# Four layers on one core: Newton's steps in PSUM, the sums' reciprocals as a tenth tap, and a ring of four pools

## The chip, the cores and the metric

The kernel runs on one core of a Trainium2 chip. The metric is the device time of that core in microseconds, as the median of several runs. One execution more was taken with the hardware profiler; all lines of a profile come from it. The engines are TensorE (PE; its weight loads are listed as PEld), VectorE (DVE), ScalarE (ACT), GpSimd (POOL) and SyncE (SP), whose queue issues the DMAs here.

## The reference

Two images of 512 channels and 64 x 64 points pass through four layers; each layer normalises its input by groups, computes, and adds the result to what came in. The change touches the first and the third.

```
x = x + L0(gn(x));  x = x + L1(gn(x));  x = x + L2(gn(x));  x = x + L3(gn(x))

def L0(x):                                # 8 heads of 64, window 3 x 3
    q = x @ W_q + b_q;  k_l, v_l = split(x @ W_kv + b_kv)
    q_norm = q / max(|q|, 1e-12);  k_l = k_l / max(|k_l|, 1e-12)     # per head
    q_scaled = (q_norm + query_embedding) * softplus(temperature)
    attn_local = q_scaled . (k_l at the 9 taps around the point)
    attn_pool  = q_scaled . normalised keys of 256 pooled tokens
    a_local, a_pool = softmax([attn_local, attn_pool])               # one sum for both
    lt = q_norm . learnable_tokens + learnable_bias + a_local
    xo = sum over 9 taps(lt * v_l at the tap) + a_pool . v_pool
    return xo @ W_proj + b_proj

def L2(x):
    gap = mean of x over the points
    s = relu(relu(gap @ w1 + b1) @ w2 + b2)          # one number per channel
    pools = [max over k x k windows of x for k in (1, 3, 5, 7, 9, 11, 13)]
    return the two pools next to s, mixed linearly, + x
```

## The kernel before

Both images run the same program one after the other: 128 channels or tokens lie on the partitions, and the four channel chunks of an image are tiles of 128 x 4096. All matmuls are in float32. Instructions of one engine run in the order in which the program was written down; a tile framework adds the semaphores between engines.

**First layer, class Local.** The work is cut into 16 units, a chunk of 128 channels (two heads) by 1024 points each. A loop over units puts the stages of neighbouring units side by side: `projections` (keys four units ahead, queries three, values one), `norms` for what was projected in the round before, `tap_products` and `tap_sums` for the next unit, `attend` for the present one, `weigh` for the one before. Each stage is a generator; `in_turn` calls them in turn, one step up to the next `yield` from each, and this fixes the order on every engine by hand. The tile pool "mm" has five PSUM banks, which `bank()` hands out to all stages.

In `norms`, four matmuls sum squares by head (L2003), ScalarE copies the rows (L2006), TensorE transposes them (L2010), and VectorE computes the inverse square root of 128 x 32 numbers: a bound below (L2013), a first guess by integer shift and multiply (L2017, L2018), a factor (L2019), and three Newton steps of three instructions (L2021, L2022, L2024); the last writes into the tile `wide`. TensorE transposes `wide` back (L2029). `normed` spreads the result over channels (L2043) and multiplies keys and queries (L2051).

In `attend`, exponentials of the scores against the pooled tokens go to `values` (L2146; GpSimd adds pairs of them, L2151) and to `sums` (L2158, L2162), whose reciprocals VectorE writes into `recip` (L2183). `el` holds the exponentials of the nine tap scores in rows of 32 per head and tap; it is multiplied by the reciprocals and the learned part is added (L2186, L2187). It then goes to DRAM, and every tap's row is fetched back, repeated over the 64 channels of its head (`fetch_tap`, L2200), because a row must meet channels that lie on the partitions.

In `weigh`, the attention over the pooled tokens, `out`, is first multiplied by the reciprocals, spread by two matmuls (L2213, L2216). Then for each of nine taps ScalarE copies the fetched rows into two PSUM banks (L2223), VectorE multiplies the shifted values by them and writes into the tap's buffer (L2226), and GpSimd adds the buffer to `out` (L2230). Three tap buffers go round: tap k + 3 is fetched when tap k is added. At the end `out` is stored to DRAM (`yd`, L2236).

**Third layer.** `pool_weights` takes group means and variances of the four chunks (L87 to L99, with GpSimd's power for the inverse root), the gap, two small matmuls (L647, L653) and almost 40 small VectorE instructions for the mixture of each channel (L656 to L680). `pool_chunk` builds the six pools of a chunk, each from the one before: a 3 x 3 maximum is a horizontal one into `h` and a vertical one into `p` (`spread_max`, L692, with an edge copy by ScalarE, L693; the first pool needs two more, L1161 and L1163). Two `h` and two `p` go round. TensorE adds each pool to eight PSUM banks by a matmul with a diagonal matrix (`add`, L1151 and L1153), which needs the mixture.

Of the kernel before, what the change touches and what calls it, by code (L numbers as in the profile page):

```python
# [15 lines left out]
P = 128  # L16
C = 512
KC = C // P
W = 64
# [38 lines left out]
class General:  # L58
# [578 lines left out]
    def pool_weights(self, X, w1, w2, sp, pp, mv=None):  # L637
# [6 lines left out]
        nc.vector.tensor_tensor(gap, gap, rstd, ALU.mult)  # L644
        ps = pp.tile([P, TB], F32, name="mm")
# [34 lines left out]
        nc.vector.tensor_scalar(c0, c0, 1.0, None, ALU.add)  # L680
# [247 lines left out]
class Net(General):  # L928
# [208 lines left out]
    def pool_weights(self, X, w1, w2, sp, pp):  # L1137
        return super().pool_weights(X, w1, w2, sp, pp, self.mv)

    def pool_chunk(self, X, Y, cc, c0, d0, wts, sp, ppa):  # L1140
# [5 lines left out]
        tmp = [Y[:, i, :].rearrange("p (y x) -> p y x", x=W) for i in range(KC)]  # L1146
# [10 lines left out]
        for j in range(1, 7):  # L1157
            h, p = tmp[j % 2], tmp[2 + j % 2]
            if j == 1:
                self.spread_max(h, img, 2)  # L1160
                nc.vector.tensor_tensor(h, h, img, ALU.max)  # L1161
                self.spread_max(p, h, 1)
                nc.vector.tensor_tensor(p, p, h, ALU.max)  # L1163
            else:

                self.spread_max(h, tmp[2 + (j - 1) % 2], 2)
                self.spread_max(p, h, 1)
            add(wts[:, j, cc:cc + 1], Y[:, 2 + j % 2, :], j)
# [491 lines left out]
class Local:  # L1660
# [332 lines left out]
    def norms(self, streams, ended):  # L1993
# [15 lines left out]
        for t in range(NT):  # L2009
            nc.tensor.transpose(ps[:, t * P:(t + 1) * P], rows[:, t * P:(t + 1) * P],  # L2010
                                self.net.ident)
        n, y, a = (wp.tile([P, NT, 4, 2], F32, name=f"norms{i}") for i in range(3))
        nc.vector.tensor_scalar(n, ps.rearrange("p (t s r) -> p t s r", t=NT, s=4)[:, :, :, :2],  # L2013
                                1e-24, None, ALU.max)
        yield

        nc.vector.tensor_scalar(y.bitcast(I32), n.bitcast(I32), 1, None, ALU.logical_shift_right)  # L2017
        nc.vector.tensor_scalar(y.bitcast(I32), y.bitcast(I32), -1, 0x5f3759df, ALU.mult, ALU.add)  # L2018
        nc.vector.tensor_scalar(n, n, -0.5, None, ALU.mult)  # L2019
        for i in range(3):  # L2020
            nc.vector.tensor_tensor(a, y, y, ALU.mult)  # L2021
            nc.vector.tensor_tensor(a, a, n, ALU.mult)  # L2022
            dst = self.wide.rearrange("p t (s r) -> p t s r", s=4)[:, :, :, :2] if i == 2 else y
            nc.vector.scalar_tensor_tensor(dst, a, 1.5, y, ALU.add, ALU.mult)  # L2024
        yield
# [97 lines left out]
    def attend(self, u):  # L2123
# [67 lines left out]
        self.fetch_tap(0)  # L2191
        yield
        self.fetch_tap(1)
        yield

    def fetch_tap(self, k):

        at = 32 * (k % 2) + 2 * k
        for h in range(2):
            self.nc.sync.dma_start(self.taps[k % 3][h * HD:(h + 1) * HD, :],  # L2200
                                   bcast(self.spread[at + h], 0, HD))

    def weigh(self, u):
# [3 lines left out]
        out, R = self.out.pop(u), self.recip  # L2207
        self.fetch_tap(2)
        yield
        banks = [self.bank() for _ in range(2)]  # L2210
        for j, ps in enumerate(banks):
            q = slice(64 * j, 64 * j + 2)
            nc.tensor.matmul(ps, self.cst[q, C_ROW:C_ROW + P], R[q, :], start=True, stop=True)  # L2213
        for j, ps in enumerate(banks):
            o = out[:, j * TB:(j + 1) * TB]
            nc.vector.tensor_tensor(o, o, ps, ALU.mult)  # L2216
        for k in range(9):
            dy, dx = divmod(k, 3)
            parts = [self.taps[k % 3][:, j * TB:(j + 1) * TB] for j in range(2)]

            banks = [self.bank() for _ in range(2)]
            for ps, part in zip(banks, parts):
                nc.scalar.copy(ps, part)  # L2223
            for j, (ps, part) in enumerate(zip(banks, parts)):
                y = y0 + dy + j * self.UY // 2
# [4 lines left out]
            nc.gpsimd.tensor_tensor(out, out, self.taps[k % 3], ALU.add)  # L2230
            if k + 3 < 9:
                self.fetch_tap(k + 3)
            if k < 8:
# [165 lines left out]
```

## Time and profile before

| | us |
|---|---|
| median of 10 runs | 5610.08 (5604.83 to 5619.77) |
| the profiled execution | 5608.33 |
| its span, first to last instruction | 5606.5 |
| first layer, image 1 and image 2 | 0 to 1148, 2800 to 3929 |
| third layer, image 1 and image 2 | 1625 to 1907, 4408 to 4690 |
| TensorE's granted clock, mean | 0.961 of full speed |

All times inside the profile are counted from the start of the span, so the span is compared with positions, and the profiled execution's own time with the runs. In a line of the timeline stand the start, the duration, the engine, the line of the kernel, the operation, the tiles written and read, and in brackets how long the engine had been idle and who released it. A row can take several instructions together ("x4").

### The profile page before, as it was taken

The numbers are of one execution on the slowest core, as the hardware profiler recorded it, in microseconds if no ns is written. First come the engines' busy times: TensorE is split into PE (matmuls) and PEld (weight loads), VectorE is DVE, ScalarE is ACT, GpSimd is POOL, SyncE is SP. The second block draws the span as 40 slices with busy tenths as digits, with TensorE's granted clock in tenths as the row PEclk, the third lists the DMA queues.
The fourth block names the chain that finished last, engine by engine and source line by source line (L and its number), as shares of the span: only waits on it lengthen the run. The fifth ranks groups of instructions, "written<-read, shape, count | busy, mean of one in ns | idle before, by whom it ended". The sixth has DMA issues, their size and how long they took to land.

```text
span 5606.5 us, 51804 instructions
## 1 busy us (share of the span) xinstructions
PE 5240.1 (93%) x19291; PEld 2263.0 (40%) x19291; DVE 3176.3 (57%) x3816; ACT 1790.4 (32%) x3413; POOL 1812.2 (32%) x1196
## 2 busy tenths in 40 slices
PE   7899999999978899999998999989999789999999
PEld 4333332554323444544343332325543334445443
DVE  3257777745669633544432677777456695334444
ACT  1245555333212233212212455542332122332221
POOL 0025555501310045444400455554013101453443
PEclk9899999999989999999998999999999899999999
DMA  3024444500000000200010344454000000000000
GB/s 137 0 64 118 123 114 136 167 21 24 1 1 0 1 1 1 76 19 34 31 51 2 87 114 116 115 148 143 17 24 1 1 0 1 1 8 14 18 15 24
DMA packets 103354, 276.37 MB, mean 49 GB/s; under 512 B 15091, under 2 KB 28147, under 8 KB 101045
## 3 DMA queue, kind: packets, MB, share of 16 engines
q1 hardware_dynamic: 103092, 272.97, 16.6%
q8 instruction: 154, 2.52, 0.2%
q14 instruction: 108, 0.88, 0.1%
HBM read 224.68 MB, written 48.23 MB: 49 GB/s over the span
## 4 chain that ended last, share of the span: by engine, by line
PE 72%; DVE 15%; issue 5%; DMA 3%; POOL 2%; ACT 2%; SPq 0%; DVEq 0%; POOLq 0%; ACTq 0%
PE mm L133 25%; DVE big L692 6%; PE mm L1330 4%; PE mm L1615 4%; PE mm L1370 4%; PE mm L547 4%; PE mm L1226 2%; PE mm L1410 2%; PE psO L1242 2%; PE psO L1602 2%; PE mm L1933 2%; PE mm L1631 2%; PE tap L2104 2%; DVE big L2226 2%; POOL late L2230 1%
## 5 line engine op out<-in xcount | busy, mean ns | idle before, releaser
L133 PE MATMUL mm<-big,w 128*128 128x512 f32 x2560 | 1200.2, 613 | 6.6 <-DVE late L2183 5.1
L133 PEld LDWEIGHTS mm<-big,w 128*128 128x128 f32 x2560 | 470.1, 193 | 708.6 <-issue 602.2
L2230 POOL TENSOR_TENSOR late<-late,big 128x1024 f32<-128x1024 f32 x192 | 454.4, 2367 | 335.7 <-DVE big L2226 332.2
L1153 PE MATMUL acc<-big,dg 128*128 128x512 f32 x896 | 408.7, 615 | 79.2 <-DVE big L692 51.2
L692 DVE TENSOR_TENSOR big<-big 128x3968 f32<-128x3968 f32 x96 | 410.8, 4289 | 39.0 <-ACT big L693 17.2
L1232 POOL TENSOR_TENSOR total<-prob 128x512 f32<-128x512 f32 x128 | 159.7, 1269 | 759.5 <-ACT prob L1229 759.5
L1584 POOL TENSOR_SCALAR qf_sum<-qf,ksum_ratio 128x512 f32<-128x512 f32 x128 | 199.1, 1564 | 552.0 <-ACT qf L1634 351.5
L1405 POOL TENSOR_TENSOR big<-big 128x512 f32<-128x512 f32 x224 | 277.5, 1271 | 235.4 <-ACT big L1396 235.4
L2151 POOL TENSOR_TENSOR late<-late 128x512 f32<-128x512 f32 x128 | 160.7, 1277 | 503.1 <-ACT late L2140 477.8
L1609 DVE RECIPROCAL k<-psD 128x512 f32<-128x512 f32 x64 | 214.9, 3357 | 184.8 <-PE psD L1606 184.8
L1153 PEld LDWEIGHTS acc<-big,dg 128*128 128x128 f32 x896 | 174.0, 197 | 312.4 <-issue 283.4
L2223 ACT COPY mm<-big 128x512 f32<-128x512 f32 x384 | 221.7, 594 | 198.8 <-DMA big<-rows 105.9
L1396 ACT ACTIVATE big<-mm,ed 128x256 f32<-128x256 f32 x512 | 194.2, 490 | 276.5 <-DVE top L1392 248.7
L2226 DVE TENSOR_TENSOR big<-big,mm 128x512 f32<-128x512 f32 x384 | 252.4, 680 | 30.4 <-ACT mm L2223 26.9
L2230 POOL TENSOR_TENSOR late<-late,tap 128x1024 f32<-128x1024 f32 x96 | 228.1, 2376 | 123.1 <-DVE norms L2024 72.3
L1330 PE MATMUL mm<-proj,k 64*128 64x256 f32 x2048 | 265.1, 391 | 0.9 <-ACT k L1297 0.9
L1249 DVE RECIPROCAL recip<-psD 128x512 f32<-128x512 f32 x64 | 214.9, 3358 | 87.1 <-PE psD L1246 87.1
L2091 DVE TENSOR_TENSOR prod<-qs,big 128x1024 f32<-128x1024 f32 x192 | 230.9, 1218 | 42.9 <-PE tap L2104 42.6
L1551 DVE TENSOR_REDUCE tops<-mm 128x2 f32<-128x512 f32 x256 | 159.4, 681 | 163.4 <-PE mm L1330 163.3
L1229 ACT ACTIVATE prob<-mm 128x512 f32<-128x512 f32 x256 | 132.0, 604 | 364.4 <-PE mm L1226 359.2
L1330 PEld LDWEIGHTS mm<-proj,k 64*128 64x128 f32 x2048 | 207.6, 188 | 95.0 <-issue 78.7
L1615 PE MATMUL mm<-k,w 128*128 128x512 f32 x512 | 235.6, 602 | 0.0
(352 smaller groups left out, 8388.8 us busy)
## 6 DMA issues: line engine op xcount, KB each, us to landing
big<-rows SPq DMA_DIRECT2D x384, 256.0 KB, 4.0
tap<-rows SPq DMA_DIRECT2D x192, 256.0 KB, 4.0
yd<-late SPq DMA_DIRECT2D x32, 512.0 KB, 4.1
out<-big SPq DMA_DIRECT2D x64, 256.0 KB, 2.0
big<-in_W_kv SPq DMA_DIRECT2D x8, 1024.0 KB, 5.9
rows<-late SPq DMA_DIRECT2D x64, 128.0 KB, 2.4
big<-yd SPq DMA_DIRECT2D x16, 512.0 KB, 4.0
big<-in_x SPq DMA_DIRECT2D x4, 2048.0 KB, 7.6
```

The costliest lines, as they stand in the source:

```text
L133: self.nc.tensor.matmul(ps, w[:, kc, :], X[:, kc, blk * TB:(blk + 1) * TB], start=(kc == 0), stop=(kc == KC - 1))
L547: nc.tensor.matmul(ps, w[:, kc, oc * P:(oc + 1) * P], att[:, kc, :], start=(kc == 0), stop=(kc == KC - 1))
L692: nc.vector.tensor_tensor(o, a, b, ALU.max)
L1153: nc.tensor.matmul(accs[b], dg, src[:, b * TB:(b + 1) * TB], start=(j == 0), stop=(j == 6))
L1330: nc.tensor.matmul(pS[h][i][:, t, :], k[lo:lo + HD, tok:tok + P], proj[lo:lo + HD, :], start=True, stop=True)
L1370: nc.tensor.matmul(ps, X[:, kc, lo:lo + P], wv[:, kc, :], start=(kc == 0), stop=(kc == KC - 1))
L1405: nc.gpsimd.tensor_tensor(a, a, part, ALU.add)
L1615: nc.tensor.matmul(ps, self.wo[:, kc, oc * P:(oc + 1) * P], qs[:, kc, :], start=(kc == 0), stop=(kc == KC - 1))
L2091: self.nc.vector.tensor_tensor(self.prods[k % 3].rearrange("p (y x) -> p y x", x=W), qs, self.kx[:, y + dy:y + dy + self.UY, dx:dx + W], A ...
L2223: nc.scalar.copy(ps, part)
L2226: nc.vector.tensor_tensor(part.rearrange("p (y x) -> p y x", x=W), self.vx[:, y:y + self.UY // 2, dx:dx + W], ps.rearrange("p (y x) -> p y ...
L2230: nc.gpsimd.tensor_tensor(out, out, self.taps[k % 3], ALU.add)
```

## The change

The change has three parts. Line numbers after it are those of the new file.

- *Newton's steps.* The transposes' PSUM bank keeps `n` and the scratch values `a`; only `y` (now `roots`) lies in SBUF. Each of the twelve instructions has at most one operand in SBUF to read. The steps are now L2050 to L2058, written one `yield` earlier; the transposes are L2043, the way back L2064. The product of `y`, `y` and `n` is formed as `(n * y) * y`, formerly `(y * y) * n`.
- *Reciprocals of the sums.* Row 20 of `el` belongs to no tap: its score is the sum of nothing, its exponential 1 and its learned part 0, so after L2221 it holds the reciprocal itself. `fetch_tap` now counts ten rows a unit, i = 0 being this one; `weigh` multiplies `out` by it (L2252 copies, L2257), and the matmuls L2213 go. Buffers go round over all units, (10 u + i) % 3, and `fetch_tap(u, 0)` and `(u, 1)` stand where taps 0 and 1 stood.
- *Third layer.* `pool_weights` computes the statistics by ScalarE instructions on single columns, two group matmuls and GpSimd's power, instead of VectorE's. The mixture itself is the same code (`pool_mixture`). The pools go round over four buffers, three of the other image's tile and one new, with a single `h`; and in the first chunk the maxima from the second pool on are written behind the last instruction of the mixture (`issue_after`).

In the compiled program the order of instructions differs only in these two layers. In the first layer the tap sums of TensorE are grouped in longer runs, and on SP's queue the store of `yd` stands before the first fetch of the next unit.

```diff
@@ -642,6 +642,11 @@
         gap = sp.tile([P, KC], F32, name="gap")
         nc.vector.tensor_tensor(gap, mv[:, :, 0], nmean, ALU.add)
         nc.vector.tensor_tensor(gap, gap, rstd, ALU.mult)
+        return self.pool_mixture(gap, nmean, rstd, w1, w2, sp, pp)
+
+    def pool_mixture(self, gap, nmean, rstd, w1, w2, sp, pp):
+
+        nc, vec = self.nc, self.vec
         ps = pp.tile([P, TB], F32, name="mm")
         for kc in range(KC):
             nc.tensor.matmul(ps[:32, :1], w1[:, kc, :], gap[:, kc:kc + 1], start=(kc == 0),
@@ -677,7 +682,7 @@
         nc.vector.tensor_tensor(d0, d0, rstd, ALU.mult)
         nc.vector.tensor_tensor(wts, wts, bcast(rstd, 1, 7), ALU.mult)
         nc.vector.tensor_tensor(c0, wts[:, 0], rstd, ALU.add)
-        nc.vector.tensor_scalar(c0, c0, 1.0, None, ALU.add)
+        self.mixed = nc.vector.tensor_scalar(c0, c0, 1.0, None, ALU.add).ins
         return c0, d0, wts
 
     def spread_max(self, out, in_, axis):
@@ -1135,7 +1140,28 @@
         return w
 
     def pool_weights(self, X, w1, w2, sp, pp):
-        return super().pool_weights(X, w1, w2, sp, pp, self.mv)
+
+        nc, mv = self.nc, self.mv
+        nmean, cent, var, rstd, gap = (sp.tile([P, KC], F32, name=f"pool_{n}")
+                                       for n in ("nmean", "cent", "var", "rstd", "gap"))
+        col = lambda a, kc: a[:, kc:kc + 1]
+        eps = sp.tile([P, 1], F32, name="pool_eps")
+        nc.gpsimd.memset(eps, 1e-5)
+        ps = pp.tile([P, TB], F32, name="mm")
+        nc.tensor.matmul(ps[:, :KC], self.grp, mv[:, :, 0], start=True, stop=True)
+        nc.scalar.mul(nmean, ps[:, :KC], -1.0)
+        for kc in range(KC):
+            nc.scalar.activation(col(cent, kc), mv[:, kc, 0:1], AF.Identity, bias=col(nmean, kc))
+        nc.scalar.activation(var, cent, AF.Square)
+        for kc in range(KC):
+            nc.scalar.activation(col(var, kc), col(var, kc), AF.Identity, bias=mv[:, kc, 1:2])
+        ps = pp.tile([P, TB], F32, name="mm")
+        nc.tensor.matmul(ps[:, :KC], self.grp, var, start=True, stop=True)
+        nc.scalar.activation(var, ps[:, :KC], AF.Identity, bias=eps)
+        nc.gpsimd.tensor_tensor(rstd, var, self.mhalf[:, :KC], ALU.pow)
+        for kc in range(KC):
+            nc.scalar.mul(col(gap, kc), col(cent, kc), col(rstd, kc))
+        return self.pool_mixture(gap, nmean, rstd, w1, w2, sp, pp)
 
     def pool_chunk(self, X, Y, cc, c0, d0, wts, sp, ppa):
 
@@ -1143,7 +1169,10 @@
         nc = self.nc
         x2 = X[:, cc, :]
         img = x2.rearrange("p (y x) -> p y x", x=W)
-        tmp = [Y[:, i, :].rearrange("p (y x) -> p y x", x=W) for i in range(KC)]
+        if cc == 0:
+            self.pools = [Y[:, i, :] for i in range(1, KC)] + [sp.tile([P, N], F32, name="pool4")]
+        image = lambda a: a.rearrange("p (y x) -> p y x", x=W)
+        h = image(Y[:, 0, :])
         accs = [ppa.tile([P, TB], F32, name="acc") for b in range(NB)]
 
         def add(w, src, j):
@@ -1155,7 +1184,8 @@
 
         add(c0[:, cc:cc + 1], x2, 0)
         for j in range(1, 7):
-            h, p = tmp[j % 2], tmp[2 + j % 2]
+            flat = self.pools[(6 * cc + j) % KC]
+            p = image(flat)
             if j == 1:
                 self.spread_max(h, img, 2)
                 nc.vector.tensor_tensor(h, h, img, ALU.max)
@@ -1163,9 +1193,12 @@
                 nc.vector.tensor_tensor(p, p, h, ALU.max)
             else:
 
-                self.spread_max(h, tmp[2 + (j - 1) % 2], 2)
-                self.spread_max(p, h, 1)
-            add(wts[:, j, cc:cc + 1], Y[:, 2 + j % 2, :], j)
+
+                with self.tc.issue_after(self.mixed) if cc == 0 else nullcontext():
+                    self.spread_max(h, last, 2)
+                    self.spread_max(p, h, 1)
+            last = p
+            add(wts[:, j, cc:cc + 1], flat, j)
         mv = self.mv[:, cc]
         if cc == KC - 1:
 
@@ -2009,19 +2042,21 @@
         for t in range(NT):
             nc.tensor.transpose(ps[:, t * P:(t + 1) * P], rows[:, t * P:(t + 1) * P],
                                 self.net.ident)
-        n, y, a = (wp.tile([P, NT, 4, 2], F32, name=f"norms{i}") for i in range(3))
-        nc.vector.tensor_scalar(n, ps.rearrange("p (t s r) -> p t s r", t=NT, s=4)[:, :, :, :2],
-                                1e-24, None, ALU.max)
-        yield
-
-        nc.vector.tensor_scalar(y.bitcast(I32), n.bitcast(I32), 1, None, ALU.logical_shift_right)
-        nc.vector.tensor_scalar(y.bitcast(I32), y.bitcast(I32), -1, 0x5f3759df, ALU.mult, ALU.add)
+
+
+        sums = ps.rearrange("p (t s r) -> p t s r", t=NT, s=4)
+        n, a = (sums[:, :, :, 2 * i:2 * i + 2] for i in range(2))
+        y = wp.tile([P, NT, 4, 2], F32, name="roots")
+        nc.vector.tensor_scalar(n, n, 1e-24, None, ALU.max)
+        nc.vector.tensor_scalar(a.bitcast(I32), n.bitcast(I32), 1, None, ALU.logical_shift_right)
+        nc.vector.tensor_scalar(y.bitcast(I32), a.bitcast(I32), -1, 0x5f3759df, ALU.mult, ALU.add)
         nc.vector.tensor_scalar(n, n, -0.5, None, ALU.mult)
         for i in range(3):
-            nc.vector.tensor_tensor(a, y, y, ALU.mult)
-            nc.vector.tensor_tensor(a, a, n, ALU.mult)
+            nc.vector.tensor_tensor(a, n, y, ALU.mult)
+            nc.vector.tensor_tensor(a, a, y, ALU.mult)
             dst = self.wide.rearrange("p t (s r) -> p t s r", s=4)[:, :, :, :2] if i == 2 else y
             nc.vector.scalar_tensor_tensor(dst, a, 1.5, y, ALU.add, ALU.mult)
+        yield
         yield
         yield
         ps = self.bank()
@@ -2188,49 +2223,49 @@
         self.spread = self.rows()
         for j in range(2):
             nc.sync.dma_start(self.spread[:, j * TB:(j + 1) * TB], el[j * HD:(j + 1) * HD, :])
-        self.fetch_tap(0)
-        yield
-        self.fetch_tap(1)
-        yield
-
-    def fetch_tap(self, k):
-
-        at = 32 * (k % 2) + 2 * k
+        self.fetch_tap(u, 0)
+        yield
+        self.fetch_tap(u, 1)
+        yield
+
+    def fetch_tap(self, u, i):
+
+
+        at = 32 * ((i - 1) % 2) + 2 * (i - 1) if i else 20
+        t = self.taps[(10 * u + i) % 3]
         for h in range(2):
-            self.nc.sync.dma_start(self.taps[k % 3][h * HD:(h + 1) * HD, :],
-                                   bcast(self.spread[at + h], 0, HD))
+            self.nc.sync.dma_start(t[h * HD:(h + 1) * HD, :], bcast(self.spread[at + h], 0, HD))
 
     def weigh(self, u):
 
         nc = self.nc
         cc, y0 = u // self.UN, u % self.UN * self.UY
-        out, R = self.out.pop(u), self.recip
-        self.fetch_tap(2)
-        yield
-        banks = [self.bank() for _ in range(2)]
-        for j, ps in enumerate(banks):
-            q = slice(64 * j, 64 * j + 2)
-            nc.tensor.matmul(ps, self.cst[q, C_ROW:C_ROW + P], R[q, :], start=True, stop=True)
-        for j, ps in enumerate(banks):
-            o = out[:, j * TB:(j + 1) * TB]
-            nc.vector.tensor_tensor(o, o, ps, ALU.mult)
-        for k in range(9):
-            dy, dx = divmod(k, 3)
-            parts = [self.taps[k % 3][:, j * TB:(j + 1) * TB] for j in range(2)]
+        out = self.out.pop(u)
+        self.fetch_tap(u, 2)
+        yield
+        for i in range(10):
+            t = self.taps[(10 * u + i) % 3]
+            parts = [t[:, j * TB:(j + 1) * TB] for j in range(2)]
 
             banks = [self.bank() for _ in range(2)]
             for ps, part in zip(banks, parts):
                 nc.scalar.copy(ps, part)
+            dy, dx = divmod(i - 1, 3)
             for j, (ps, part) in enumerate(zip(banks, parts)):
+                if i == 0:
+                    o = out[:, j * TB:(j + 1) * TB]
+                    nc.vector.tensor_tensor(o, o, ps, ALU.mult)
+                    continue
                 y = y0 + dy + j * self.UY // 2
                 nc.vector.tensor_tensor(
                     part.rearrange("p (y x) -> p y x", x=W),
                     self.vx[:, y:y + self.UY // 2, dx:dx + W],
                     ps.rearrange("p (y x) -> p y x", x=W), ALU.mult)
-            nc.gpsimd.tensor_tensor(out, out, self.taps[k % 3], ALU.add)
-            if k + 3 < 9:
-                self.fetch_tap(k + 3)
-            if k < 8:
+            if i:
+                nc.gpsimd.tensor_tensor(out, out, t, ALU.add)
+            if i + 3 < 10:
+                self.fetch_tap(u, i + 3)
+            if 0 < i < 9:
                 yield
         lo = u % self.UN * self.UT
         nc.sync.dma_start(self.yd[:, cc, lo:lo + self.UT], out)
```

## The prediction

> **What bounds the kernel now.** I read the shares of busy time first, then the chain of waits by engine, then stretches of one stage, and last the timeline of one period. From the page:
>
> ```profile
> PE 5240.1 (93%) x19291; PEld 2263.0 (40%) x19291; DVE 3176.3 (57%) x3816; ACT 1790.4 (32%) x3413; POOL 1812.2 (32%) x1196
> PE 72%; DVE 15%; issue 5%; DMA 3%; POOL 2%; ACT 2%; SPq 0%; DVEq 0%; POOLq 0%; ACTq 0%
> ```
>
> TensorE carries the end, except for a seventh of the chain that lies on VectorE. The stretches (columns: PE, PEld, DVE, ACT, POOL busy, granted clock, DMA share, GB/s) say where:
>
> ```profile
> 600.00:700.00 100.00, 95.04 (x338) 30.94 (x336) 71.72 (x100) 53.13 (x93) 52.51 (x26) 1.00 0.46 125
> 1700.00:1800.00 100.00, 82.42 (x180) 35.05 (x179) 98.71 (x31) 33.31 (x96) 0.00 (x0) 0.93 0.00 0
> ```
>
> The first is the first layer: TensorE is busy 95%, so only removed TensorE work, or the missing 5%, pays. The second is the third layer: VectorE is full and TensorE is not.
>
> In the first layer a period lasts 48.3 us (603.84 to 652.16, two starts of L2003). Its one visible TensorE stall is L2029 waiting for the last Newton step; the list of waits sums it, and the timeline shows its making:
>
> ```profile
> PE mm L2029 <- DVE wide L2024: 71.3, 30, 3.2
> 605.89 1.13 PE L2213 MATMUL mm<-late,cst 2*128 2x512 f32 x4
> 610.75 1.27 DVE L2017 TENSOR_SCALAR norms<-norms 128x32 int32<-128x32 int32 x1
> 612.02 3.52 SPq L2200 DMA_DIRECT2D big<-rows  x4
> 613.08 1.38 DVE L2018 TENSOR_SCALAR norms<-norms 128x32 int32<-128x32 int32 x1
> 617.43 2.23 DVE L2022 TENSOR_TENSOR norms<-norms,norms 128x32 f32<-128x32 f32 x1
> 620.71 0.63 PE L2029 MATMUL mm<-cst,wide 128*128 128x128 f32 x4 [2.26 <-DVE wide L2024]
> ```
>
> The same shape takes 0.17 to 0.19 us in other places (L2022 min, median, max: 174, 191, 2240 ns). Three steps are stretched by 1.1, 1.2 and 2.0 us, each beside an addition of POOL (L2230). In the third layer:
>
> ```profile
> 1652.69 5.12 POOL L99 TENSOR_TENSOR gn_rstd<-gn_var,cst 128x4 f32<-128x4 f32 x1 [42.44 <-DVE gn_var L97]
> 1666.23 0.40 ACT L1151 ACTIVATE dg<-cst,pw_c 128x128 f32<-128x128 f32 x1 [7.27 <-DVE pw_c L680]
> 1683.43 8.69 DVE L692 TENSOR_TENSOR big<-big 128x3968 f32<-128x3968 f32 x2 [17.23 <-ACT big L693]
> ```
>
> The statistics queue among 4.3 us maxima (L97 done at 1652.6, POOL's power blocked to 5.12 us), so the first diagonal comes at 1666.2. By then both pools of the ring are written, and VectorE stands idle 17.2 us until TensorE has read one.
>
> **What the Trainium skill says.** "SBUF — State Buffer", section "Who interferes with whom": VectorE and GpSimd share a port pair as an exclusive lock; an operation with two SBUF inputs, or in a two-port mode, blocks or is blocked whole. The trace agrees (1.27, 1.38, 2.23 us against 0.17 to 0.19; POOL's power 5.12 against 1.01 at 1909.26). "VectorE: DVE Perf Modes", section "Why PSUM operands drop a tier": the two-port mode needs both SBUF read ports, so a PSUM operand excludes it. The trace agrees as far as it goes: L2013, which reads PSUM, never takes over 0.193 us. "TensorE: Matmul & The Clock Gate", section "The mechanism" (packing): matmuls on different column groups run concurrently. Here four tap sums at 637.42 to 637.45 last 0.59 us each, side by side.
>
> **A, Newton's steps in PSUM.** The twelve instructions stay; each now has at most one SBUF input. The stretch of about 1.1+1.2+2.0 = 4.4 us of VectorE time a period should go; I bound it by 0 and 4.4, and take 4.4. That alone doesn't give PE 2.26 us, because VectorE runs in order and other work stands among the steps. One bank of five is held for some 12 us instead of about 1; the compiled order puts no TensorE wait on its release, but four banks rotate faster. I price that at 0 to 1 us and take 0, since the matmuls that wait for a bank wait for copies and products, as before.
>
> **B, the sums' reciprocals.** L2213 goes: four instructions, 1.06 to 1.13 us of TensorE a period. In its place comes a tenth tap: two DMAs on SP's queue, two ScalarE copies (L2223: 594 ns, so 1.2 us); the two VectorE products remain (L2216, 0.68 each); POOL adds nothing. Sums over a period are about 30 us on VectorE, 27 on ScalarE and 25 on POOL, all below 48, so throughput is covered; latency isn't. SP issues the store of yd (which waits for POOL's last addition) now ahead of tap 0's fetch, formerly after taps 0 and 1. Tap 0 is first wanted at the next period's start; walked with ten taps, the last addition comes early enough to leave it some 2.5 us, an estimate.
> In the new order the tap sums of TensorE also stand in longer runs: pieces of 1.0, 0.97, 1.07, 1.16, 1.82 and 0.97 us (7.0) become about 1.8, 1.2, 2.0 and 1.0 (6.0).
>
> **One period walked**, T = 0 at L2003, now L2036, by durations of the old rows. ScalarE copies tap 0 by 3.9; the second product ends at 4.9, and L2043 (the transposes, formerly L2010) waits for the first: hidden by exponentials and values. Tap 1's products end at 6.1. POOL, busy to 5.4 with L2151, adds it at 6.2 to 8.6. That releases the fetch of tap 4, which by the old rows lands 4.6 us on (the queue's landing is 4.0), at 13.2. Its product on VectorE (14.0 to 14.6) stands in order before the last Newton steps and the product for tap sum 7 (15.0 to 16.1); "wide" is ready at 16.2, against 16.7 in the old period. TensorE's idle time there stays near 1.9 us, since the work ahead of it has shrunk too. The rest of the period is 28.7 instead of 31.5, two more tap-sum runs having moved forward. 17.2 + 28.7 = 45.9: **2.4 us saved a period** = 1.06 (L2213) + 1.0 (runs) + 0.35 (idle).
> Thirteen periods an image have this form, so 31 us. The last units have no projections to cover a tenth tap: about 3 us for tap 0 behind the store and 3 for the tenth tap (a ninth of the last unit's 38.4 us is 4.3, partly covered), so +6 an image; the three units there without L2213 give -3, and the three before them, outside the thirteen, -3. Net 0. L2024's two early rounds (a bare chain of 12 steps) don't change.
>
> **C, the third layer.** VectorE now does only four maxima before the mixture. The chain from the last aggregate (1635.2): two group matmuls and the mixture's two (0.56 three times, 1.86 once: 3.5), fifteen small ScalarE operations at 0.17 to 0.25, say 0.25 with the step between them (3.8), L650 0.25, POOL's power 1.0 since VectorE is idle then, and nine hand-overs of some 0.1. That is 9.5 us: L656 (now L661) starts at about 1644.8. In the compiled order it stands before the fourth maximum (L1163, now L1193: 4.42), which then fills 1645.0 to 1649.4; the mixture's 5.1 us of small steps end at 1654.5. 52 maxima of 4.383 with their neighbours give 1882.4. Before: 49 of them from 1683.43 end at 1898.2. **15.7 us saved an image**, bounds 10 and 18 (chain 3 us shorter, 6 longer). TensorE's seven additions of 6.9 us (48) stay under VectorE's 61 a chunk, and four pools keep it from stalling; late next is VectorE itself. The last addition and layer 3's loads, already issued, do not move.
>
> **Sum.** Per image 31.2 + 0 + 15.7 = 46.9, twice 93.8. Against the profiled execution's 5608.33 (span 5606.5 and 1.8 around it): 5514.5. That execution lies 1.75 below the median of 5610.08, so the median may be 5516; I give 5514. TensorE's granted clock dips in places (L2043 takes 2.08 at 915.64, 1.13 elsewhere), worth some 10 us either way.
>
> **Rivals.**
> - *The stall goes entirely.* For: nothing but in-order products stands between Newton's steps. Against: tap 4's landing. The period is 48.3 - 1.06 - 1.0 - 2.26 = 44.0, saving 4.3 x 13 = 56 an image; with C, 5608.3 - 2 x 71.6 = 5465.
> - *The first layer gives nothing:* PSUM operands don't free Newton's steps, or the read-back at the period's start takes back what L2213 gave. For: L2043 now waits for a DMA, a copy and a product instead of one matmul. The period stays 48.3, the tail costs 3: 5608.3 - 2 x 12.7 = 5583.
> - *Slower: the loop of the taps becomes the bound.* A tap's buffer goes round fetch, copy, product, addition; nine took 38.4 us in the last unit (1079.08 to 1117.46), so ten take 42.7, with the yd store now in line at SP. If each tap costs 5.1 beside full queues, the period is 51: 13 x 2.7 + 3 - 15.7 = +22 an image, 5653. It decides from a period of 49.3 on (13 x 1.0 + 3 outweighs C). Against: no engine is near that.
>
> **How the numbers follow.** The sum 0.55, stall gone 0.17, first layer nothing 0.20, loop of taps 0.06; 0.02 for a cancellation near zero. The range, 5460 to 5585, takes in the second and third case. About 0.2% (11 us) is what a measurement of this kernel can tell from no change: faster 0.92, within it 0.02, slower 0.06.
>
> **What would show it.** Right: L2051 and L2052 at 0.2 us; period near 45.9 with L2064's idle time near 1.9; tap 4's copy just after 13 us; POOL's power near 1.0 us and the first diagonal near 1654.5; the third layer's maxima ending some 16 us earlier against the layer's start. Wrong: L2043 idle for L2257, the yd store late on SP's queue, TensorE waiting for banks, a period of 48 or more, or an idle gap left in the third layer after the mixture.

## The result, and the profile after

The changed kernel takes 5513.81 us in the median of 8 runs (5509.66 to 5525.13). Its ratio to the kernel before is 0.9828, 95% interval 0.9819 to 0.9837. The forecast was 5514; the profiled execution took 5512.22, with a span of 5510.4. The sum came out almost exactly, but by luck: terms of the first layer were wrong in both directions, and some 34 of the 98 us come from drops of TensorE's clock that went away, which stood in the sum only as an uncertainty.

From the page after, the shares of busy time:

```profile
PE 5184.8 (94%) x19163; PEld 2256.7 (41%) x19163; DVE 3054.0 (55%) x3804; ACT 1831.1 (33%) x3505; POOL 1804.8 (33%) x1198
```

VectorE's busy time fell by 122 us with only 12 instructions fewer: the stretch of Newton's steps is gone (a steady period has 31.25 us of VectorE work, before 35.8). TensorE's busy time fell by 55 us, part of it time at a lower clock. One steady period of the first layer, which is the time from one start of the squares to the next, as a stretch of the changed kernel (columns as before: length, then busy time and instructions of PE, PEld, DVE, ACT, POOL, granted clock, DMA share, GB/s):

```profile
398.51:444.56 46.05, 44.40 (x161) 14.54 (x160) 31.25 (x50) 26.88 (x47) 26.26 (x13) 1.00 0.53 137
```

The period is 46.06 us (forecast 45.9, before 48.3), and TensorE waits once in it, for 1.65 us. The list of waits (who waited for whom: us in total, times, longest) says for what:

```profile
PE tap L2139 <- DVE prod L2126: 40.8, 31, 1.9
PE mm L2064 <- DVE wide L2058: 11.8, 6, 3.1
```

TensorE no longer waits for `wide` in the steady periods: of the six waits left, four belong to the early rounds (1.9 and 3.1 us in each image) and two, of 0.85, to the last period with less work. It now waits for a tap product instead. The timeline of the period that begins at 583.72:

```profile
589.80 0.19 DVE L2050 TENSOR_SCALAR mm<-mm 128x32 f32<-128x32 f32 x1
590.50 0.19 DVE L2051 TENSOR_SCALAR mm<-mm 128x32 int32<-128x32 int32 x1
591.20 0.18 DVE L2052 TENSOR_SCALAR roots<-mm 128x32 int32<-128x32 int32 x1
593.88 0.69 DVE L2260 TENSOR_TENSOR tap<-big,mm 128x512 f32<-128x512 f32 x1 [1.26 <-ACT mm L2252]
596.94 0.59 ACT L2252 COPY mm<-big 128x512 f32<-128x512 f32 x1 [0.40 <-DMA big<-rows]
599.22 1.21 DVE L2126 TENSOR_TENSOR prod<-qs,big 128x1024 f32<-128x1024 f32 x1
600.35 0.18 DVE L2058 SCALAR_TENSOR_TENSOR wide<-mm,roots 128x32 f32<-128x32 f32 x1
600.49 1.05 PE L2139 MATMUL tap<-prod,cst 128*32 128x512 f32 x4 [1.65 <-DVE prod L2126]
601.47 0.66 PE L2064 MATMUL mm<-cst,wide 128*128 128x128 f32 x4
```

The integer steps take 0.19 and 0.18 us. Tap 4 is copied at 596.94, 13.2 after the squares, as forecast; `wide` is ready at 16.8, where 16.2 was forecast and 16.7 was the old value. Though no step is stretched any more, it comes no earlier: between the first step (L2050) and the last (L2058) VectorE does nine products of other stages and waits 1.26 us for ScalarE, where before it did six products and never waited. In the third layer:

```profile
1605.58 1.02 POOL L1161 TENSOR_TENSOR pool_rstd<-pool_var,cst 128x4 f32<-128x4 f32 x1 [3.76 <-ACT pool_var L1160]
1610.09 0.16 DVE L661 TENSOR_TENSOR pw_s<-mm,vec 128x4 f32<-128x4 f32 x1 [4.42 <-PE mm L658]
1619.62 13.08 DVE L697 TENSOR_TENSOR big<-big 128x3968 f32<-128x3968 f32 x3
1619.75 0.40 ACT L1180 ACTIVATE dg<-cst,pw_c 128x128 f32<-128x128 f32 x1 [4.67 <-DVE pw_c L685]
```

The power takes 1.02 us instead of 5.12. The layer's first maximum starts at 1591.16, so the first diagonal comes 28.6 us after it, before the change 41.4; VectorE goes on at once and waits for no pool.

Positions in the two traces, image 1, give the account (us):

| part | before | after | difference |
|---|---|---|---|
| up to the first steady period | 352.64 | 352.45 | -0.2 |
| twelve periods, squares to squares | 591.0 | 548.2 | -42.8 |
| last squares to the last output matmul | 200.8 | 207.9 | +7.1 |
| second layer, to the first maximum | 480.4 | 482.6 | +2.2 |
| first to last maximum | 273.2 | 258.5 | -14.7 |
| sum | | | -48.4 |

Half of the span's difference is 48.05. The forecast had 31.2 for the periods, 0 for the tail and 15.7 for the third layer, 46.9 in all. The second layer's part lies between 480 and 483 in all profiles of these kernels.

The 42.8 of the periods are of two kinds. Eleven full periods are 2.28 shorter each, 25.1 together, of which one longer period after takes back 1.0; the twelfth, with less TensorE work, is some 2.2 shorter at full clock. The other 16.5 are drops of TensorE's granted clock before: 11.0 in three periods of 53.10, 53.10 and 49.81 (clock 0.90, 0.90 and 0.97), and 5.5 in the twelfth. Its stretch before, and the same one in image 2 of experiment 10, whose first layer is the same but whose clock didn't fall there:

```profile
895.32:943.67 48.35, 44.28 (x150) 12.62 (x149) 36.89 (x50) 23.45 (x41) 26.26 (x13) 0.86 0.43 125
3697.89:3740.71 42.82, 38.59 (x149) 12.07 (x148) 36.70 (x50) 23.37 (x41) 26.30 (x13) 1.00 0.49 141
```

In image 2 the periods gave 46.1, of which 17.2 are drops of the clock, counted in the same way; the tail lost 3.7 there.

### The profile page after: what moved, and what is told of

Its sections match the earlier page's. It is cut to its first block, busy times and chain, and to the rows that moved or that the text cites. A ratio compares the mean times of both kernels' runs of the same rounds, so it can differ in the third digit from the quotient of the medians.

```text
span 5510.4 us, 51859 instructions
## 1 busy us (share of the span) xinstructions
PE 5184.8 (94%) x19163; PEld 2256.7 (41%) x19163; DVE 3054.0 (55%) x3804; ACT 1831.1 (33%) x3505; POOL 1804.8 (33%) x1198
## 5 line engine op out<-in xcount | busy, mean ns | idle before, releaser
L133 PE MATMUL mm<-big,w 128*128 128x512 f32 x2560 | 1186.7, 609 | 5.8 <-DVE late L2218 5.1
L1182 PE MATMUL acc<-big,dg 128*128 128x512 f32 x704 | 317.7, 608 | 58.3 <-DVE big L697 27.8
L697 DVE TENSOR_TENSOR big<-big 128x3968 f32<-128x3968 f32 x72 | 308.8, 4289 | 6.6 <-DVE big L697 0.5
L2252 ACT COPY mm<-big 128x512 f32<-128x512 f32 x428 | 244.2, 596 | 144.3 <-DMA big<-rows 106.2
L2139 PE MATMUL tap<-prod,cst 128*32 128x512 f32 x768 | 198.7, 601 | 41.3 <-DVE prod L2126 40.8
```

The lines of the kernel that those rows point to most:

```text
L133: self.nc.tensor.matmul(ps, w[:, kc, :], X[:, kc, blk * TB:(blk + 1) * TB], start=(kc == 0), stop=(kc == KC - 1))
L697: nc.vector.tensor_tensor(o, a, b, ALU.max)
L1182: nc.tensor.matmul(accs[b], dg, src[:, b * TB:(b + 1) * TB], start=(j == 0), stop=(j == 6))
```

## The experiments

Twelve runs follow, of eleven kernels. Ratios are against the kernel before, with 95% intervals.

**1. Newton's steps alone.** Only the part of the diff in `norms` is applied.

```diff
-        n, y, a = (wp.tile([P, NT, 4, 2], F32, name=f"norms{i}") for i in range(3))
+        n, a = (sums[:, :, :, 2 * i:2 * i + 2] for i in range(2))
+        y = wp.tile([P, NT, 4, 2], F32, name="roots")
...
```

> The kernel before with Newton's steps in PSUM and nothing else. Theory 1 (the steps' stretch in SBUF makes VectorE late at wide): the integer steps fall to 0.2 us, TensorE's wait for wide drops from 2.3 to about 1 us in each of the thirteen periods of an image, and the clock drops that follow the long waits (about 11 us an image in the profile before) go: 2 x (13 x 1.3 + 11) = 56 us, ratio near 0.990. Rival (what is last ahead of wide is the fetch of a tap, whatever the steps take): the period stays within 0.3 us of 48.3, under 8 us in all, or about 25 with the clock drops gone; ratio 0.996 to 0.999.

Measured: 5520.64 us, ratio 0.984 (0.9823 to 0.9856). This single part brings nearly all of the change. A period of its trace as a stretch, then the first and the last of the steps and their use in another period, which begins with the squares at 535.00:

```profile
393.43:439.30 45.87, 45.75 (x167) 14.75 (x164) 31.62 (x50) 25.92 (x47) 26.21 (x13) 1.00 0.48 127
```

```profile
540.62 0.19 DVE L2017 TENSOR_SCALAR mm<-mm 128x32 f32<-128x32 f32 x1
547.24 0.19 DVE L2025 SCALAR_TENSOR_TENSOR wide<-mm,roots 128x32 f32<-128x32 f32 x1
549.54 0.66 PE L2031 MATMUL mm<-cst,wide 128*128 128x128 f32 x4
```

The same two steps in the profile before (squares at 603.84):

```profile
609.46 0.18 DVE L2013 TENSOR_SCALAR norms<-mm 128x32 f32<-128x32 f32 x1
620.37 0.19 DVE L2024 SCALAR_TENSOR_TENSOR wide<-norms,norms 128x32 f32<-128x32 f32 x1
```

In both kernels the first step starts 5.6 us after the squares, six products stand among the steps, and VectorE waits for nothing up to the last. That one starts 12.2 us after the squares, against 16.5 before: the whole stretch reached `wide`. TensorE uses it 2.3 us later and is busy for the whole period, L2213 included. The period is 45.86, shorter than the full change's, and no full period shows a drop of the clock; of the 93 us gained, the drops make some 34. Theory 1 had the direction right but the size too small by two fifths (56 us against 93): it left TensorE a wait of 1 us, and put the drops at 11 us an image. The rival fell.

**2. The tenth tap alone.** Only the parts in `attend`, `fetch_tap` and `weigh`.

```diff
-            nc.tensor.matmul(ps, self.cst[q, C_ROW:C_ROW + P], R[q, :], start=True, stop=True)
+        for i in range(10):
...
```

> The kernel before with the reciprocals read back as a tenth tap, Newton's steps left in SBUF, third layer as before. Theory 1 (each first-layer part needs the other): L2213's 1.06 us and the tap sums' 1.0 us leave TensorE, but wide is no earlier, so that the wait for it grows by as much, to about 4 us; the last units lose some 7 us an image: ratio 0.998 to 1.005. Rival (removed TensorE work pays by itself): 2 x (13 x 2.06 - 7) = 40 us, ratio near 0.993.

Measured: 5591.38 us, ratio 0.9956 (0.9939 to 0.9972), between the two theories and just better than theory 1's end. The period is 47.82, only 0.5 less, though 1.4 us of TensorE work are gone (44.4 us busy, before 45.8). Three waits take the place of one, of 1.4, 1.0 and 1.1 us in a period; the first two from the list of waits, the third from the timeline of the period that begins at 497.44:

```profile
PE tap L2104 <- DVE prod L2091: 37.1, 27, 1.6
PE mm L2029 <- DVE wide L2024: 35.5, 30, 2.8
519.59 3.70 PE L133 MATMUL mm<-big,w 128*128 128x512 f32 x8 [1.08 <-DVE tap L2225]
```

The tail grows to 212.4 and 213.4 us in the two images (200.8 and 202.8 before). In image 1 eleven shorter periods give 6, the absent drops of the clock 16.5 (11 in the full periods, 5.5 in the twelfth, which lasts 42.8 instead of 48.35), and the tail takes 11.6: 11 us gained, and 22 were measured for two images. Without the clock, by these figures, the tenth tap alone would lose some 6 us an image, an estimate.

**3. The third layer alone.** All of the diff outside class Local.

```diff
+        return self.pool_mixture(gap, nmean, rstd, w1, w2, sp, pp)
+            self.pools = [Y[:, i, :] for i in range(1, KC)] + [sp.tile([P, N], F32, name="pool4")]
+                with self.tc.issue_after(self.mixed) if cc == 0 else nullcontext():
...
```

> The kernel before with the third layer's part alone. Theory 1: 14.7 us an image as between the two profiles, 29 in all, ratio 0.9948. Rival (the gain shows only with the first layer's other pace, or the fourth layer gives some back through its loads): under 20 us, ratio over 0.9965.

Measured: 5579.94 us, ratio 0.9939 (0.9922 to 0.9955). The maxima last 258.5 and 258.6 us, as in the full change, against 273.2 and 272.3. Theory 1 holds; the fourth layer gives nothing back (from image 2's last maximum to the end 926.5 us, before 926.4).

**4. All but Newton's steps.** The changed kernel with the old `norms`.

```diff
-        n, a = (sums[:, :, :, 2 * i:2 * i + 2] for i in range(2))
-        y = wp.tile([P, NT, 4, 2], F32, name="roots")
+        n, y, a = (wp.tile([P, NT, 4, 2], F32, name=f"norms{i}") for i in range(3))
...
```

> The changed kernel with Newton's steps put back into SBUF, at their old place. Theory 1: the first layer's period returns to about 48, since the stretched steps make wide late again; the third layer's 29 us stay: ratio against before near 0.995. Rival (Newton's steps are a side matter once L2213 is gone): within 10 us of the changed kernel, ratio near 0.984.

Measured: 5566.27 us, ratio 0.9916 (0.99 to 0.9933). The period is 47.82, as in experiment 2. Put back, the steps cost some 50 us. Theory 1 has the period right and the ratio wrong: the drops of the clock don't come back, every full period stands at a clock of 1.00. The medians don't add: the parts alone gain 93, 22 and 34, together 149, and the whole gains 98. Each of the two first-layer parts alone ends the drops of the clock, so that some 34 us are counted twice. The other 17 fit what the waits show: steps and tenth tap compete for the same idle time of TensorE.

**5 and 6. All but the tenth tap**, run twice.

```diff
-        for i in range(10):
+            nc.tensor.matmul(ps, self.cst[q, C_ROW:C_ROW + P], R[q, :], start=True, stop=True)
...
```

> Newton's steps in PSUM and the third layer's part, with the matmuls L2213 kept and no tenth tap. Theory 2 (formed after the four runs before: Newton's steps alone end the wait for wide, and the tenth tap then takes as much as it gives): the first layer's period is 45.9 us with TensorE never waiting, the last units lose nothing, the third layer gains 14.3 an image: 5516.6 - 28 = 5489 of span, ratio near 0.979, faster than the changed kernel. Rival (the parts share one gain, and the whole change is the best of them): at or above the changed kernel, ratio 0.983 or more.

> Newton's steps in PSUM and the third layer's part without the tenth tap, once more for a narrower interval. Theory 2: ratio near 0.979, below the changed kernel's 0.9828 by more than both intervals. Rival (the tenth tap neither costs nor gives): within 0.001 of 0.9828.

Measured: 5501.53 us, ratio 0.9798 (0.9769 to 0.9827), and in the second run 5497.74 us, ratio 0.9802 (0.9788 to 0.9815). The second interval lies below that of the changed kernel (0.9819 to 0.9837): **this version beats the changed kernel**, by some 15 us. Its traces say where: periods of 45.86 instead of 46.06 (2 us an image), and tails of 202.6 and 200.2 in the first run, of 199.4 and 199.9 in the second, instead of 207.9 and 206.5 (5 to 9 us an image).

**7. An earlier `wide`.** The changed kernel, with tap 3's products behind the last Newton step.

```diff
-            nc.vector.scalar_tensor_tensor(dst, a, 1.5, y, ALU.add, ALU.mult)
+            self.newton = nc.vector.scalar_tensor_tensor(dst, a, 1.5, y, ALU.add, ALU.mult).ins
...
+                with self.net.tc.issue_after(self.newton) if i == 3 else nullcontext():
+                    nc.vector.tensor_tensor(
...
```

> The changed kernel with one order more: VectorE's products of the third tap are issued behind the last Newton step, so that wide comes early and L2064 stands before seven of the tap sums on TensorE. Theory 2 (what holds the tenth tap's gain back is TensorE's new wait of 1.65 us for the product of tap sum 7): the period falls from 46.06 to about 44.4, 2 x 12 x 1.65 = 40 us, ratio near 0.975. Rival (the tap loop, 2 to 3 us later at its third tap, reaches the next period's start late): the period stays at 46 or grows, and L2043 waits for L2257; ratio 0.982 or more.

Measured: 5535.61 us, ratio 0.9854 (0.9823 to 0.9884), no gain; the period is 46.77. From its timeline (this period's squares start at 500.88):

```profile
512.90 1.97 PE L2171 MATMUL mm<-big,kp 64*128 64x512 f32 x4
513.65 0.19 DVE L2058 SCALAR_TENSOR_TENSOR wide<-mm,roots 128x32 f32<-128x32 f32 x1
513.75 0.29 PEld L2171 LDWEIGHTS mm<-big,kp 64*128 64x128 f32 x2 [0.55 <-ACT big L2110]
515.78 0.65 PE L2064 MATMUL mm<-cst,wide 128*128 128x128 f32 x4
521.87 1.05 PE L2139 MATMUL tap<-prod,cst 128*32 128x512 f32 x4 [0.67 <-DVE prod L2126]
```

`wide` is 3.9 us earlier than in the full change and the wait for tap sum 7 falls from 1.65 to 0.67. But TensorE is busy 1.7 us longer in a period, at a clock of 1.00: L2171 takes 1.97 instead of 1.13, as the second half of it, with its weight load, comes only after ScalarE's L2110, and the tap sums, in six runs instead of five, take 0.85 more. The tails are 212.4 and 211.3, longer too. Theory 2 fell; the rival has the outcome but not its reason, as L2043 doesn't wait for L2257.

**8. The store of `yd` on GpSimd's queue**, in the changed kernel.

```diff
-        nc.sync.dma_start(self.yd[:, cc, lo:lo + self.UT], out)
+        nc.gpsimd.dma_start(self.yd[:, cc, lo:lo + self.UT], out)
```

> The changed kernel with the store of yd issued by GpSimd, behind its own last addition, instead of standing before tap 0's fetch on SP's queue. Theory 2 (the 6 to 7 us that the last units lose are tap 0's fetch behind the store): the tail from the last squares to the last output matmul falls from 207 by 3 to 7 us an image, and the periods don't change: ratio 0.980 to 0.982. Rival (the loop of ten taps itself is longer): tail within 1.5 us of 207, ratio 0.983.

Measured: 5526.93 us, ratio 0.9839 (0.9808 to 0.9869), which can't be told from the changed kernel's. The tails are 209.3 and 209.5. Theory 2 fell: the tail doesn't shrink. It is 1.4 and 3.0 us longer, so that the rival's 1.5 isn't met in image 2, but its reason fits what the full change's last unit shows (timeline):

```profile
1038.75 2.39 SPq L2237 DMA_DIRECT2D big<-rows  x4
1041.18 0.58 SPq L2271 DMA_DIRECT2D yd<-late  x1
1045.25 1.11 ACT L2252 COPY mm<-big 128x512 f32<-128x512 f32 x2 [9.55 <-DMA big<-rows]
1047.21 3.81 PE L1966 MATMUL mm<-sq,big 128*128 128x512 f32 x4 [8.09 <-DVE late L2257]
```

In the last unit the first fetch stands ahead of the store anyway. What TensorE waits for, 8.1 us, is the way through DRAM: 6.5 us from issue to copy, then the product. Before, two matmuls spread the reciprocals and the same wait was 4.4 us. From its first fetch to its store (1080.54) this unit takes 41.8 us, before 38.4. That is 3.4 of the 7.1 us that image 1's tail lost; where the rest lies isn't shown.

**9. Both orders together.**

```diff
+                with self.net.tc.issue_after(self.newton) if i == 3 else nullcontext():
...
+        nc.gpsimd.dma_start(self.yd[:, cc, lo:lo + self.UT], out)
```

> Both orders together: VectorE's third tap behind the last Newton step, and the store of yd issued by GpSimd. Theory 2: the gains of the two add, period 44.4 and a tail of 200 to 204; ratio 0.972 to 0.975. Rival (the tap loop decides): if the third tap's delay is what binds the period, the freed queue gives some of it back, and this kernel is better than the one with the third tap's order alone by more than the tail's 7 us.

Measured: 5549.68 us, ratio 0.9886 (0.9857 to 0.9916), period 46.77, tails 214.6 and 214.1. The interval lies above the changed kernel's. The two orders don't help each other: experiment 7 alone has the same period and shorter tails.

**10. The ring of four alone**, in the kernel before.

```diff
-            h, p = tmp[j % 2], tmp[2 + j % 2]
+            flat = self.pools[(6 * cc + j) % KC]
+            p = image(flat)
...
```

> The kernel before with the ring of four pools and the single h alone; the statistics stay on VectorE among the maxima. Theory 2 (the ring moves the idle time, the early mixture ends it): eleven maxima now stand before or within the mixture, which ends near 1681 instead of 1666; TensorE has read the first pool near 1696, so VectorE still idles some 14 us: 6 us saved an image, ratio near 0.998. Rival (the ring of two was the whole stall): 14 us an image or more, ratio 0.995.

Measured: 5622.88 us, ratio 1.0016 (1.0007 to 1.0026). It loses 10 us; the maxima last 274.9 and 274.8 us, 2 more than before. One line of its timeline:

```profile
1704.35 17.51 DVE L692 TENSOR_TENSOR big<-big 128x3968 f32<-128x3968 f32 x4 [16.53 <-PE acc L1156]
```

With more pools to write, more maxima stand ahead of the mixture, the first diagonal moves from 41 to 55 us after the first maximum (1632.7 to 1687.85), and VectorE waits 16.5 us for TensorE as it waited 17.2. The rival fell; theory 2's idle time is about right, its gain is not. The longer maxima make 4 us of the 10; the rest isn't placed. Parts that no experiment changed vary as much between these profiles: the start up to the first squares between 205 and 218 us, and the part from image 1's last maximum to image 2's first squares between 1094 and 1104.

**11. Statistics and order without the ring of four.**

```diff
-            flat = self.pools[(6 * cc + j) % KC]
-            p = image(flat)
+            flat = Y[:, 2 + j % 2, :]
+            h, p = image(Y[:, j % 2, :]), image(flat)
```

> The kernel before with ScalarE's statistics and the maxima behind the mixture, but two h and two pools going round. Theory 2: the mixture is ready at the fourth maximum, so TensorE (6.9 us a pool) reads faster than VectorE writes (8.8), and a ring of two costs about 1 us once: 13 us an image, ratio near 0.995. Rival (both are needed): VectorE waits in the first chunk for a free pool as before, 5 us an image or less, ratio 0.998 or more.

Measured: 5586.89 us, ratio 0.9953 (0.9939 to 0.9967). The maxima last 260.5 and 259.0 us: 12.6 and 13.3 us gained, so the early mixture is the cause, and the ring adds the last 0.4 to 2. ScalarE's statistics and the order behind the mixture were not tried apart, so which of them makes the mixture early stays open. One wait for a pool is left in each image, 4.57 and 3.04 us:

```profile
1678.47 21.93 DVE L697 TENSOR_TENSOR big<-big 128x3968 f32<-128x3968 f32 x5 [4.57 <-PE acc L1179]
```

**12. Newton's operands back in SBUF.** From experiment 5's kernel; only `n` stays in PSUM.

```diff
-        n, a = (sums[:, :, :, 2 * i:2 * i + 2] for i in range(2))
+        n, a = sums[:, :, :, :2], wp.tile([P, NT, 4, 2], F32, name="scratch")
...
-        nc.vector.tensor_scalar(y.bitcast(I32), a.bitcast(I32), -1, 0x5f3759df, ALU.mult, ALU.add)
+        nc.vector.tensor_scalar(y.bitcast(I32), y.bitcast(I32), -1, 0x5f3759df, ALU.mult, ALU.add)
...
-            nc.vector.tensor_tensor(a, n, y, ALU.mult)
-            nc.vector.tensor_tensor(a, a, y, ALU.mult)
+            nc.vector.tensor_tensor(a, y, y, ALU.mult)
+            nc.vector.tensor_tensor(a, a, n, ALU.mult)
```

> As the kernel with Newton's steps in PSUM and the third layer's part, but with only n left in PSUM: the second integer step reads and writes SBUF, y times y and the last instruction of a step have two inputs in SBUF. Theory 2 (operations in SBUF are stretched wherever POOL is adding): the second integer step, y times y of the first step, or both take over 1 us, wide is 1 to 4 us later than the 12.2 us after the squares that it has in that kernel, and from about 4 us on TensorE waits again; ratio 0.980 to 0.985. Rival (the order and not the place of the operands freed the steps): all twelve stay at 0.2 us, ratio as of the next kernel.

Measured: 5545.84 us, ratio 0.9888 (0.9873 to 0.9904), 48 us above the kernel that it starts from. One period of its timeline (squares at 634.27), POOL's additions among the steps:

```profile
640.05 2.36 POOL L2265 TENSOR_TENSOR late<-late,big 128x1024 f32<-128x1024 f32 x1 [0.44 <-DVE big L2261]
640.80 1.65 DVE L2052 TENSOR_SCALAR roots<-roots 128x32 int32<-128x32 int32 x1
644.21 0.17 DVE L2056 TENSOR_TENSOR scratch<-scratch,mm 128x32 f32<-128x32 f32 x1
647.55 2.41 POOL L2265 TENSOR_TENSOR late<-late,tap 128x1024 f32<-128x1024 f32 x1 [2.02 <-DVE scratch L2056]
647.77 2.23 DVE L2055 TENSOR_TENSOR scratch<-roots 128x32 f32<-128x32 f32 x1
650.61 0.63 PE L2064 MATMUL mm<-cst,wide 128*128 128x128 f32 x4 [1.72 <-DVE wide L2058]
```

The integer step from SBUF to SBUF ends at 642.45, 0.04 after POOL's addition ends at 642.41; the product of two SBUF inputs ends at 650.00, again 0.04 after POOL at 649.96. POOL adds once more between these two, from 643.18 to 645.54: there L2056, with one input in PSUM, runs 0.17 us in the midst of the addition, while L2058 (644.90, 0.69 us), with both tensors in SBUF, ends 0.05 after it. Together 4.0 us of the stretch are back. The last step starts 16.0 us after the squares (12.2 in experiment 5), TensorE waits 1.72 us, and the period is 47.8. So the place of the operands sets it: the steps are written in the same order as in experiment 5. The Trainium skill, "SBUF — State Buffer", section "Who interferes with whom", says that a VectorE instruction with at most one SBUF input, outside the two-port modes, doesn't contend with GpSimd, and this trace agrees. The loss was larger than expected, and all of it lies in the periods (24.5 and 24.0 us in the two images).

## Why the prediction was right, and where it was not

**A, right in mechanism, wrong in its effect.** The stretch of 4.4 us went as taken, and experiment 12 brings 4.0 of it back by moving operands alone. The sentence "That alone doesn't give PE 2.26 us, because VectorE runs in order and other work stands among the steps" is the step that failed. It does give it: `wide` came 4.3 us earlier (16.5 to 12.2), TensorE's wait ended, and the period fell to 45.86 by this part alone (experiment 1). The profile before could have told: from the first step to the last VectorE never waits, so that each microsecond taken from the steps reaches `wide`, as long as the same products stand among them.

**B, wrong in sign beside A.** The prediction put 2.06 of the 2.4 us a period on L2213 and the longer runs of tap sums. TensorE's work fell by only 1.4 (45.8 to 44.4 us busy): L2213's 1.06 are gone, but the tap sums take 7.1 us in five runs, before 7.2 in six, where 6.0 in four had been counted. And with the tenth tap three more products and a wait of 1.26 us stand among the steps, which take back the 4.3 us that A gave to `wide`. The period became 0.2 us longer than without B, as the 1.65 us wait for tap sum 7 came in. The walk had the place right (tap 4 at 13.2, `wide` at 16.2, measured 16.8) and an idle time of 1.9 where 1.65 was measured. What it lacked was the walk of A alone, with which B is to be compared: 45.9 there too. So the number 45.9 came out, measured 46.06, with the causes exchanged.

**The count of periods.** Thirteen of 2.4 us made 31.2. Eleven have the full form, and at full clock the periods of image 1 gave 26.

**The tail** was put at net 0 and lost 7.1 us in image 1 and 3.7 in image 2. Of its terms, tap 0 "behind the store" isn't the loss; experiment 8 frees the store and the tail doesn't shrink. The 3 us for the tenth tap are near what the last unit's loop shows (3.4). The 6 us credited for L2213 outside the thirteen periods aren't seen, neither in the tail nor ahead of the first steady period (352.64 before, 352.45 after).

**C, right.** 15.7 forecast, 14.7 and 13.8 measured in the two images; VectorE's idle time until L661 was put at 5.4 and is 4.42, while the first diagonal was put 29.6 us after the first maximum (1624.85 to 1654.5) and came at 28.6. Experiments 10 and 11 split it as the argument did not: the early mixture gives 13, the ring of four 0.4 to 2, and the ring without the early mixture nothing.

**The clock** was named as 10 us either way and stands in the sum with nothing. It gave 16.5 us in image 1 and 17.2 in image 2, because the drops are gone. Without them some 62 of the span's 96 us would be left, against 94 forecast: an estimate, but it shows that the near hit is luck. The clock made up for what the other terms fell short.

**The rivals.** The first rival's stall did go entirely, with A alone, where L2213 stays. The second rival's mechanism, a read-back that takes back what L2213 gave, is true of B beside A, but not by L2043, which never waits in the steady periods; the layer as a whole gained. The third rival's period of 49.3 was never near.

## What to carry to other kernels

Small VectorE instructions on a chain were worth moving into PSUM here, operand by operand, because GpSimd adds tensors in SBUF at the same time; look for a duration that ends when GpSimd's does. When a change has several parts that aim at one wait, walk each alone as well as all together: the second may find nothing left, and cost its own latency. Count drops of the clock apart from the waits, or they are credited to every part that ends them. Here a deeper ring helped only once the work that frees it started early; that start was the thing to move.

## What the runs showed of the hardware

In the first layer's full periods TensorE's clock fell only behind waits of more than 2.2 us. In the kernel before, a 2.26 us wait for `wide` stands in each period, and behind some of them the clock falls for a while; stretches around the one that ends at 369.51:

```profile
364.00:370.00 6.00, 3.74 (x19) 1.06 (x17) 5.79 (x13) 2.67 (x5) 2.41 (x1) 1.00 0.37 105
370.00:382.50 12.50, 12.50 (x28) 3.52 (x26) 8.84 (x12) 3.19 (x6) 9.48 (x5) 0.59 0.44 121
```

Such a period lasts 53.1 us instead of 48.3. The Trainium skill, "TensorE: Matmul & The Clock Gate", section "HAM oscillation — how this bites in real kernels", asks for no idle gaps over about 3.4 us; here 2.26 us comes before the drop, and the measurement decides. The kernels of experiments 3, 10 and 11, which have the same first layer, show them too, mostly three or four periods apart. In the other kernels, whose single waits in the full periods are 2.1 us or less, every full period stands at a clock of 1.00. It isn't the sum of the idle time: a full period of experiment 2 has 3.4 us of it in three waits, before 2.5, and no drop. But the length of one wait isn't the whole condition either: in the twelfth period of experiment 2, whose waits are 1.4 us or less, the clock is 0.96. That the wait for `wide` is the cause of the drops was not tried by itself; these profiles agree with it.

The order written in the kernel isn't quite the order on the engine, other than said above. The changed program writes Newton's twelve steps in one piece, and in the trace nine products of other stages stand between them. Where it was moved by hand (experiment 7), one wait shrank and others came.
